# The ninth step of a layer 1 batch: each product of the next k ahead of its mixing

## The chip, the core and the metric

The kernel runs on one core of a Trainium2 chip. The metric is the device time of one execution in microseconds (us). The core has five engines with an instruction queue each: TensorE (PE; its weight loads are listed apart as PEld), VectorE (DVE), ScalarE (ACT), GpSimd (POOL) and SyncE (SP), which here only issues transfers (DMA). An engine works through its queue in the order in which the program gives it, and waits at an instruction until the semaphores that it names have been reached. Work in SBUF is fed to TensorE, whose results stand in PSUM until another engine takes them away.

## The reference, cut to what matters

Eight images of 512 channels and 1024 positions go through two attention layers. The change lies in layer 1, which is computed batch by batch, a batch being one image:

```python
xf = x.reshape(b, c, t)                                  # c = 512, t = 1024, after a group norm
q = jnp.einsum('oc,bct->bot', w_q, xf).reshape(b, heads, hd, t)      # 8 heads of 64
k = jnp.einsum('oc,bct->bot', w_k, xf).reshape(b, heads, hd, t)
v = jnp.einsum('oc,bct->bot', w_v, xf).reshape(b, heads, hd, t)
attn = jnp.einsum('bhdq,bhdT->bhqT', q, k) * scale
attn = jnp.einsum('gh,bhqT->bgqT', w_head, attn)         # the heads are mixed
attn = jax.nn.softmax(attn, axis=-1)
mean, var = moments of attn over both last axes
attn = (attn - mean) / jnp.sqrt(var + EPS) * in_gamma + in_beta
out = jnp.einsum('bhqT,bhdT->bhqd', attn, v).reshape(b, t, c) @ w_proj.T + b_proj
```

(The line of the moments is shortened.) All of it is float32. The kernel doesn't divide by the softmax sums at once: it multiplies the values with plain exponentials and brings in sums and moments later.

## The kernel before, in words

**Steps.** In layer 1 a batch has eight blocks of 128 query positions, p = 0 to 7. A block goes through four stages: its scores; their mixing over heads with the exponentials; a transpose with statistics; and the product with v ("values"). `Attention1.step(p, t, ag)` (L1847) writes out one quarter t = 0 to 3 of step p. In step p the scores of block p, the mixing of block p - 1 and the values of block p - 2 (from the third quarter on those of block p - 1) stand side by side, so that there is a ninth step, p = 8, in which there are no new scores. The order of these calls is the order of each engine's queue: it is written out by hand, and no scheduler changes it.

**One mixing.** The scores are copied from PSUM to `raw`, and `regroup` (L1642) has SyncE move them to other partitions, into `re` (L1646). `mix(p, s)` (L1656) reads `re` with matmuls on 32 x 32 tiles of the array (L1665) into two PSUM tiles of the pool `ps_m`; ScalarE then writes the exponentials `e` (L1678), one instruction for each tile. `flip` (L1693) transposes `e` into `et` on VectorE, `moments` (L1704) takes its statistics there, `values` (L1720) multiplies `et` with v on TensorE, and `leave` (L1736) takes the results away on ScalarE. `sums` (L1746 to L1750, VectorE) and `totals` (L1757, TensorE, tile `z`) make the softmax sums.

**The next k.** While a batch ends, the k of the next one is computed: 512 x 512 weights by 512 x 1024 positions, as seven block products instead of eight (a scheme of Strassen's kind). `Projection.products(m)` (L1367) issues product m as four matmuls of 128 x 128 by 512 (L1379; the profile lists eight, two for each matmul), and `leave(m)` (L1385) takes it out of PSUM: product 1 is copied to a sum `u` on ScalarE (L1388); product 2 is added on top of product 1 in the same PSUM tile, after that copy, and leaves on ScalarE as a quarter of k (L1433); product 6 is added to `u` on VectorE (L1394), product 7 makes a second sum `v` there (L1396), product 5 is added to `u` (L1400) and makes a quarter of k with `v` (L1435), as do 4 and 3. The right factors of products 5 to 7 and 4 are differences of blocks of y that VectorE makes (L1354); 0 and 1 of them are made at the end of the first quarter, 2 and 3 at the end of the second.

**The agenda.** An `Agenda` holds functions under slots, and `ag.run(slot)` calls those of a slot. The batch loop (L1922 to L1998) puts products 1, 2, 6 and 7 under 31.5, 32.5, 33.5 and 34.5, which `step` calls in the ninth step at 4p - 0.5 to 4p + 2.5. `k_go` (L1941) issues a product and notes its leaving in `due`; `k_leave` (L1441) issues what is noted at the end of the same quarter, ahead of that quarter's `flip` and `moments`. After the ninth step come product 5, the rest of the values, products 4 and 3, v, the output projection and the next q. The eighth batch has no next k, and nothing stands under these slots.

**PSUM.** The pool `ps_m` has three buffers of two banks. Scores, mixings (two each), products of projections and pairs of v take them in the order of the program; a matmul into a buffer waits until its last contents have been read. Values and `z` use another pool of two buffers.

Of the kernel before, what the change touches and what calls it, by code (L numbers as in the profile page):

```python
# [467 lines left out]
def tile_two_attention_layers(  # L468
# [228 lines left out]
    with ExitStack() as l0:  # L697
# [505 lines left out]
        for b in range(B):  # L1203
            more = b + 1 < B
            ag = Agenda()
# [61 lines left out]
    with ExitStack() as l1:  # L1267
# [173 lines left out]
        def k_leave():  # L1441
            for fn in due:
                fn()
            due.clear()
# [168 lines left out]
        class Attention1:  # L1613
# [233 lines left out]
            def step(self, p, t, ag):  # L1847

                new, old, older = p < NT, p >= 1, p >= 2
                if t == 0:  # L1850
                    if new:
                        for i in range(3):
                            self.scores(p, i)
                    if older:
                        self.values(p - 2, 0, 2, 3)
                        self.leave(p - 2, 0)
                        self.sums(p - 2)
                        if p % 2 == 0 and p >= 4:
                            self.divide(p // 2 - 2, nc.gpsimd)
                    if old:  # L1860
                        self.mix(p - 1, 0)
                    ag.run(4 * p - 0.5)
                elif t == 1:
                    if older:
                        self.values(p - 2, 1, 0)
                        self.flip(p - 1, 0)
                        self.totals(p - 2)
                        self.moments(p - 1, 0)
                    if new:
                        self.scores(p, 3)  # L1870
                    if old:
                        self.mix(p - 1, 1)
                    ag.run(4 * p + 0.5)
                elif t == 2:
                    if older:
                        self.values(p - 2, 1, 1)
                    if new:
                        self.scores(p, 4)
                        self.scores(p, 5)
                    if old and not new:  # L1880
                        self.mix(p - 1, 2)
                    ag.run(4 * p + 1.5)
                    if older:
                        self.values(p - 2, 1, 2, 3)
                        self.leave(p - 2, 1)
                    if old and new:
                        self.mix(p - 1, 2)
                else:
                    if new:
                        self.scores(p, 6)  # L1890
                        if old:
                            self.values(p - 1, 0, 0)
                        self.scores(p, 7)
                        if old:
                            self.mix(p - 1, 3)
                            self.values(p - 1, 0, 1)
                    else:
                        self.mix(p - 1, 3)
                        self.values(p - 1, 0, 0, 1)
                    ag.run(4 * p + 2.5)  # L1900
                k_leave()
                if p == 1 or old and t:
                    self.flip(p - 1, t)
                    self.moments(p - 1, t)
                if new:
                    for kh, s in (
                        (), ((0, 0), (0, 1), (0, 2)), ((0, 3),), ((1, 0), (1, 1), (1, 2), (1, 3)),
                    )[t]:
                        self.regroup(p, kh, s)
                if old and t == 0:  # L1910
                    self.piece()
                ag.run(4 * p + t)
# [9 lines left out]
        for b in range(B):  # L1922
            more = b + 1 < B
            a = Attention1(b)
            ag = Agenda()
# [143 lines left out]
```

## Time and profile before

| | |
|---|---|
| median of 3 runs | 3999.17 us (3997.65 to 4006.88) |
| the profiled execution | 3999.31 us, span 3997.5 us |
| TensorE busy | 3885.5 us, 97% of the span |
| VectorE busy | 2834.6 us, 71% |
| ScalarE busy | 1971.3 us, 49% |
| mixing, all of it (L1665) | 315.3 us busy, 19.3 us idle ahead of it |
| values, all of it (L1720) | 557.0 us busy, 12.1 us idle ahead of it |
| first matmul of product 1, first and seventh batch | 1982.95 and 3652.95 us |

A row of a timeline gives the start from the beginning of the span, the duration, engine, line, operation, the tiles written and read, the number of instructions merged in it, and in brackets how long the engine was idle ahead of it and what ended that. Matmuls are pipelined, so the end of a group overlaps the start of the next by about a tenth of a microsecond; sums are made from start to start. "PEclk" is the share of TensorE's full clock that was granted.

### The profile page before, as it was taken

The page shows a single profiled execution, that of the slowest core. Times are in us where ns is not written, and L with a number is a line of the kernel's source. Part 1 is how long each engine was busy: PE and PEld are TensorE (multiplying, and loading weights), DVE is VectorE, ACT ScalarE, POOL GpSimd, SP SyncE. Part 2 cuts the span into 40 slices and gives each one's busy share as a digit, 9 for nine tenths or more (in the row PEclk, how much of TensorE's full clock was granted, in tenths as well). Part 3 has the DMA queues.
Part 4 walks back from the last instruction along what each step waited for, and adds up shares of the span by engine and source line. Part 5 has one row for each costly group of instructions (what it writes and reads, how often), then busy time and mean ns, then how long its engine had stood idle before and what let it go on. Part 6 is the DMA issues. An engine that isn't in the chain of part 4 may idle for free.

```text
span 3997.5 us, 95841 instructions
## 1 busy us (share of the span) xinstructions
PE 3885.5 (97%) x41932; PEld 1826.1 (46%) x41932; DVE 2834.6 (71%) x4124; ACT 1971.3 (49%) x2431; POOL 128.5 (3%) x150
## 2 busy tenths in 40 slices
PE   8999999999999999999999999999999999999997
PEld 4353535344343535344544535545545445445354
DVE  4748475766657584857958949859769679588597
ACT  1726363544536271615717528437257166175274
POOL 0000000000000000000100000000001000000010
PEclk9999999999999999999999999999999999999999
DMA  3313131111121111217828749658469288397384
GB/s 121 120 48 117 46 120 48 62 59 66 53 83 54 72 68 61 75 66 184 230 92 226 190 120 237 173 137 227 148 164 228 99 210 207 97 232 198 107 219 127
DMA packets 245883, 519.10 MB, mean 130 GB/s; under 512 B 47312, under 2 KB 54480, under 8 KB 238800
## 3 DMA queue, kind: packets, MB, share of 16 engines
q1 hardware_dynamic: 238912, 497.95, 43.2%
q0 software_dynamic: 6544, 14.94, 1.7%
q8 instruction: 331, 5.42, 0.6%
q14 instruction: 96, 0.79, 0.1%
HBM read 197.16 MB, written 46.92 MB: 61 GB/s over the span
## 4 chain that ended last, share of the span: by engine, by line
PE 81%; DVE 13%; ACT 2%; DMA 2%; issue 2%; SPq 0%; DVEq 0%
PE s L1084 11%; PE a L1110 11%; PE a L1720 7%; PE s L1628 7%; DVE bn L1704 6%; PE pk_p L902 6%; PE pq_p L902 5%; PE pv L1454 5%; PE pv_p L902 5%; DVE et L1693 5%; PE pp_p L902 5%; PE pk L1379 4%; PE pq L1379 4%; PE pp L1379 4%; PE m L1665 4%
## 5 line engine op out<-in xcount | busy, mean ns | idle before, releaser
L1693 DVE STREAM_TRANSPOSE et<-e 128x2048 f32<-128x2048 f32 x256 | 587.3, 2294 | 88.7 <-ACT e L1678 86.8
L1720 PEld LDWEIGHTS a<-et,v 128*64 128x64 f32 x16384 | 509.2, 138 | 296.2 <-issue 247.6
L1704 DVE BATCH_NORM_STATS2 bn<-e 128x6 f32<-128x512 f32 x1024 | 634.3, 675 | 0.0
L1089 ACT ACTIVATE e<-s 128x1024 f32<-128x1024 f32 x512 | 497.2, 1026 | 234.5 <-PE s L1084 232.1
L1640 ACT COPY raw<-s 128x1024 f32<-128x1024 f32 x480 | 470.2, 1018 | 226.1 <-PE s L1628 197.5
L1720 PE MATMUL a<-et,v 128*64 128x64 f32 x16384 | 557.0, 225 | 12.1 <-DVE et L1693 11.4
L1678 ACT ACTIVATE e<-m 128x1024 f32<-128x1024 f32 x512 | 496.2, 1021 | 126.5 <-PE m L1665 54.2
L1097 DVE TENSOR_TENSOR zacc<-zacc,e 128x1024 f32<-128x1024 f32 x384 | 468.7, 1221 | 87.2 <-ACT e L1089 64.9
L1628 PE MATMUL s<-k,q 64*64 64x512 f32 x4096 | 516.0, 608 | 6.2 <-DVE q L1493 3.1
L1084 PE MATMUL s<-q,k 64*64 64x512 f32 x4096 | 490.1, 593 | 2.3 <-ACT e L1089 2.3
L1110 PE MATMUL a<-e,v 64*64 64x512 f32 x4096 | 484.1, 589 | 0.0
L1665 PE MATMUL m<-re,wmix 32*32 32x512 f32 x8192 | 315.3, 604 | 19.3 <-DMA re<-raw 17.8
L1110 PEld LDWEIGHTS a<-e,v 64*64 64x64 f32 x4096 | 156.7, 133 | 282.8 <-issue 282.2
L1084 PEld LDWEIGHTS s<-q,k 64*64 64x64 f32 x4096 | 147.9, 133 | 275.2 <-issue 240.7
L1628 PEld LDWEIGHTS s<-k,q 64*64 64x64 f32 x4096 | 127.7, 132 | 220.8 <-issue 78.2
L1454 PE MATMUL pv<-wv,y 128*128 128x512 f32 x480 | 212.1, 597 | 0.0
L1736 ACT COPY q<-a 64x256 f32<-64x256 f32 x256 | 93.7, 366 | 184.7 <-PE a L1720 182.7
L1772 POOL DMA_DIRECT2D zd<-rz x56 | 34.7, 619 | 3449.0 <-DVE r L1784 3449.0
L1454 PEld LDWEIGHTS pv<-wv,y 128*128 128x128 f32 x480 | 89.3, 190 | 116.9 <-issue 110.3
L1665 PEld LDWEIGHTS m<-re,wmix 32*32 32x32 f32 x8192 | 66.7, 103 | 148.9 <-ACT raw L1640 58.6
L1458 ACT COPY v<-pv 128x512 f32<-128x512 f32 x30 | 17.6, 585 | 218.7 <-PE pv L1454 218.7
L1095 DVE TENSOR_TENSOR zacc<-e,e 128x1024 f32<-128x1024 f32 x64 | 78.3, 1223 | 56.1 <-ACT e L1089 56.1
(315 smaller groups left out, 3942.4 us busy)
## 6 DMA issues: line engine op xcount, KB each, us to landing
re<-raw SPq DMA_DIRECT2D x1024, 256.0 KB
left_q<-left_q SPq DMA_DIRECT2D x17, 1792.0 KB
left_p<-left_p SPq DMA_DIRECT2D x17, 1792.0 KB
left_k<-left_k SPq DMA_DIRECT2D x10, 1792.0 KB
x<-in_x_dram SPq DMA_DIRECT2D x32, 512.0 KB
rzb<-zd SPq DMA_DIRECT2D x128, 128.0 KB
x<-x SPq DMA_DIRECT2D x64, 256.0 KB
y<-x SPq DMA_DIRECT2D x32, 512.0 KB
```

The lines of the kernel that those rows point to most:

```text
L902: nc.tensor.matmul(out, st, mv, start=start, stop=(k == 1), skip_group_check=True)
L1084: nc.tensor.matmul(ps[c * D : c * D + D, m], k[r, hp, k0 : k0 + D], q[r, hp, ts(f, FB)], start=True, stop=True,)
L1089: nc.scalar.activation(e[i], ps, AF.Exp, scale=S0 * S0)
L1110: nc.tensor.matmul(acc[g][a][m * D : m * D + D], v[rows, kc, ts(2 * hp + m, D)], e[i][rows, m], start=(kc == 0), stop=(kc == NG - 1),)
L1379: nc.tensor.matmul(self.ps[m][:, i], w[:, left, k * HC + i * P : k * HC + i * P + P], right[:, k], start=(k == 0 and m != 2), stop=(k == 1 ...
L1454: nc.tensor.matmul(ps[:, m], y_t[b][:, c, ts(2 * i + m, P)], w[:, c], start=(c == 0), stop=(c == NCC - 1),)
L1628: nc.tensor.matmul(ps[c * D : c * D + D, m], qo_t[b][r, p, hp, ts(c, D)], k_t[b][r, hp, ts(kh, FB)], start=True, stop=True,)
L1665: nc.tensor.matmul(ps[a // 2][c * 32 : c * 32 + 32, a % 2].rearrange("p (r h k) -> p h r k", r=2, h=2), wmix[rows].rearrange("p g i -> p ( ...
L1678: nc.scalar.activation(e[:, :, 2 * h : 2 * h + 2].rearrange("p r a k -> p a r k"), ps[h].rearrange("p a (r k) -> p a r k", r=2), AF.Exp,)
L1693: nc.vector.transpose(self.et[p, u].rearrange("p kb (r st a) g q -> p st kb r (a g q)", r=2, st=2)[:, st], self.e[p, s].rearrange("p r a ( ...
L1704: nc.vector.bn_stats(self.bn[p][:, s, a], e[:, :, a].rearrange("p r k -> p k r"))
L1720: nc.tensor.matmul(acc[two * D : two * D + D, s].rearrange("p (x q) -> p x q", q=4), v_t[b][:, kb, ts(g, D)], et[:, kb, :, g], start=(kb = ...
```

## The change

In the four quarters of a step the call of the agenda's slot is put ahead of the mixing. In the fourth quarter it goes ahead of the mixing and of the values behind it, and it is called in the branch without new scores alone. Slots at these places hold work in the ninth step only, so nothing else moves. `k_leave` keeps its place, and so the queues of ScalarE, VectorE, GpSimd and SyncE keep their orders.

```diff
                         if p % 2 == 0 and p >= 4:
                             self.divide(p // 2 - 2, nc.gpsimd)
+                    ag.run(4 * p - 0.5)
                     if old:
                         self.mix(p - 1, 0)
-                    ag.run(4 * p - 0.5)
                 elif t == 1:
...
                     if new:
                         self.scores(p, 3)
+                    ag.run(4 * p + 0.5)
                     if old:
                         self.mix(p - 1, 1)
-                    ag.run(4 * p + 0.5)
                 elif t == 2:
...
                         self.scores(p, 4)
                         self.scores(p, 5)
+                    ag.run(4 * p + 1.5)
                     if old and not new:
                         self.mix(p - 1, 2)
-                    ag.run(4 * p + 1.5)
                     if older:
...
                     else:
+                        ag.run(4 * p + 2.5)
                         self.mix(p - 1, 3)
                         self.values(p - 1, 0, 0, 1)
-                    ag.run(4 * p + 2.5)
                 k_leave()
```

In the ninth step TensorE's queue then reads as follows (v for the values, with the number of records that the profile shows for them):

```
before: mixing 0, product 1, v 32, z, mixing 1, product 2, v 32, mixing 2, product 6, v 64,
        mixing 3, v 64, product 7, product 5, v 192, z
after:  product 1, mixing 0, v 32, z, product 2, mixing 1, v 32, product 6, mixing 2, v 64,
        product 7, mixing 3, v 64, product 5, v 192, z
```

## The prediction

> **What bounds the kernel now.** I read the page's busy shares first, then the waits of TensorE, then the ninth step (p = 8) of the batches as a timeline, engine by engine. The shares say that TensorE is nearly always at work, so time comes only from its few waits:
>
> ```profile
> PE 3885.5 (97%) x41932; PEld 1826.1 (46%) x41932; DVE 2834.6 (71%) x4124; ACT 1971.3 (49%) x2431; POOL 128.5 (3%) x150
> L1665 PE MATMUL m<-re,wmix 32*32 32x512 f32 x8192 | 315.3, 604 | 19.3 <-DMA re<-raw 17.8
> ```
>
> The mixing waits 17.8 us in all for the transfer that regroups the scores. The first batch's ninth step on TensorE (start, duration; the bracket is idle time before it):
>
> ```profile
> 1981.87 1.15 PE L1665 MATMUL m<-re,wmix 32*32 32x512 f32 x32 [1.69 <-DMA re<-raw]
> 1982.95 3.70 PE L1379 MATMUL pk<-y,left_k 128*128 128x512 f32 x8
> 1986.58 1.15 PE L1720 MATMUL a<-et,v 128*64 128x64 f32 x32
> 1987.56 0.37 PE L1757 MATMUL z<-sel,zz 128*64 128x32 f32 x4
> 2003.45 7.13 PE L1379 MATMUL pk<-right,left_k 128*128 128x512 f32 x16
> 2010.51 5.82 PE L1720 MATMUL a<-et,v 128*64 128x64 f32 x192
> 2016.16 0.37 PE L1757 MATMUL z<-sel,zz 128*64 128x32 f32 x4
> ```
>
> Only mixing 0 waits; from there to 2016.16 TensorE has no other gap, and the chain that ended last runs along it. In the seven batches with a following one this wait is 1.69, 2.40, 1.86, 1.41, 3.29, 2.33 and 2.51 us, 15.49 us together: all that the change can take away directly. ScalarE and VectorE in the same step:
>
> ```profile
> 1983.20 1.94 ACT L1678 ACTIVATE e<-m 128x1024 f32<-128x1024 f32 x2 [2.24 <-issue]
> 1986.69 1.01 ACT L1388 COPY re<-pk 128x1024 f32<-128x1024 f32 x1 [1.55 <-PE pk L1379]
> 1993.68 2.28 DVE L1693 STREAM_TRANSPOSE et<-e 128x2048 f32<-128x2048 f32 x1
> 1998.28 1.20 DVE L1354 TENSOR_TENSOR right<-y 128x1024 f32<-128x1024 f32 x1
> 2003.90 2.45 DVE L1704 BATCH_NORM_STATS2 bn<-e 128x6 f32<-128x512 f32 x4
> 2007.19 1.22 DVE L1396 TENSOR_TENSOR re<-re,pk 128x1024 f32<-128x1024 f32 x1 [0.84 <-PE pk L1379]
> ```
>
> To be seen: the copy of product 1 (L1388) stands behind the two exponentials of mixing 0, and product 7's departure (L1396) stands at the end of a VectorE run without gaps from 1993.68 to 2006.35.
>
> **What the Trainium skill says.** "TensorE: Matmul & The Clock Gate", Part 3 (what overlaps and what doesn't): matmuls start and end strictly in program order. So what stands behind a waiting product waits too; the gapless order above agrees. The same page, Part 1 (the HAM clock gate): a free-running window of 3413 ns measures activity, and after an idle window the array runs at half clock. The trace agrees and sharpens it. The clock records hold halvings of 3.41 us or twice that; counted in windows of that length, every window of layer 1 with 1.83 us or more of TensorE idle is followed by half clock, and none with 1.74 or less:
>
> ```profile
> 2810.36:2813.77 3.41, 1.58 (x40) 1.00 1.00 255
> 2813.78:2817.18 3.40, 3.40 (x4) 0.50 1.06 242
> 3373.56:3376.97 3.41, 1.68 (x34) 1.00 0.94 241
> 3376.98:3380.38 3.40, 3.40 (x20) 1.00 1.07 249
> ```
>
> (Columns: window, length, TensorE busy, clock, DMA.) Two of the seven waits cost such a window: in the fourth batch product 1 took 5.40 us for 3.70 (1.70 lost), in the fifth mixing 0 took 1.62 for 1.15 and product 1 4.88 for 3.70 (1.65 lost).
>
> **The change part by part.** No instruction is added or removed, and the orders of ScalarE, VectorE, GpSimd and SyncE stay as they are; only TensorE's order changes, in seven of eight batches. Products 1, 2, 6 and 7 go ahead of mixings 0, 1, 2 and 3; product 7 also passes 64 values (as the trace counts them). PSUM buffers go round differently with it.
>
> I work from T = 1980.13 of the first batch, where TensorE became free, in steps from the rows' starts: product 3.63, mixing 1.07, 32 values 0.98 to 1.05, 64 values 2.02, z 0.30; mixing start to its exponentials 1.34; the pair occupies ScalarE for 1.82; copy 1.01; 0.05 to 0.15 from a releaser's end to TensorE's start, as its other waits show.
>
> *Removed.* Product 1 needs nothing that is late and covers 3.63 us; the longest wait is 3.29, so all seven go: 15.49 plus 0.05 each, 15.8 us. Without this cover they would be back in full.
>
> *Added, before product 2.* It accumulates on product 1's PSUM and so must follow the copy L1388. Until now 32 values, z and mixing 1 stood between them, 2.35 us from product 1's end (1986.58) to 1988.93, while the copy took 1986.69 to 1987.70: no wait. Now: product 1 at 0, mixing 0 at 3.63, exponentials at 4.97, copy at 6.79 to 7.80, product 2 at 7.85. TensorE has only 32 values and z after mixing 0 and is free at 5.98: a wait of 1.87. Behind it stand mixing 1, its exponentials and VectorE's transpose of them.
>
> *Added, before product 6.* Mixing 1 starts at 11.48, exponentials at 12.82; product 6's buffer comes free with the first of them at 13.84, and TensorE is free at 13.58: 0.31.
>
> *Added, before product 7.* The late exponentials end at 14.76, so the transpose at 1993.68 (13.55 from T) starts at 14.80. VectorE then needs 4.60 to its third subtraction (1993.68 to 1998.28) and 1.20 for it: 20.60, against TensorE free at 20.61: about 0.1.
>
> *Added, before product 5.* Until now its buffer came from an exponential. Now it is that of product 7, given back by L1396 on VectorE, behind the statistics of mixing 2. From the third subtraction to the end of those statistics is 8.05 (1998.28 to 2006.35 less the usual overlap): L1396 runs 27.45 to 28.67, product 5 starts at 28.75; TensorE is free at 27.42: 1.33. Behind it stand the remaining 192 values, z and the tail of the batch.
>
> *Moved.* Products 7 and 5 stood together (7.06); apart they are 7.26, 0.2 more. What one change of kind from product to mixing costs, the trace doesn't show; the nearest, product to values, is 0.2 and is in my 3.63. Four such changes a batch at a price of 0 take 0.8 us off it (5.6 in all, 4004), at 0.4, twice the nearest, they add as much (4016); I keep 0.2.
>
> Sum: z at 32.38 + 5.65 = 38.03 from T instead of 34.29 plus the old wait, so 3.75 added per batch: 7 x 3.75 = 26.2. Net 26.2 - 15.8 = +10.4 us. Nothing downstream absorbs it: after z TensorE runs without a gap through products 4 and 3, values of v, output and q.
>
> *Half clock.* The two old windows go: -3.35. The new wait before product 2 shows as 1.80 us idle, right at the threshold; it counts only if it falls whole into one window, with a chance of (3.41 - 1.80)/3.41 = 0.47. Bounds are 0 and 7 windows of 1.7 us; I take two, +3.4. Total +10.5 on the profiled execution: 3999.31 + 10.5 = 4009.8. That execution is 0.14 above the median of 3999.17 (its span 3997.5 lies 1.8 under its own time), so **4010 us**.
>
> **The rivals.**
> *The product-5 wait stays hidden.* If VectorE caught up, 1.33 x 7 = 9.3 would fall away: about 4000.5, no change. For it: VectorE is 71% busy overall. Against it: it is gapless in just this stretch.
> *More half clock.* With four or more windows, or dearer changes of kind: 4014 to 4021. For it: seven idle stretches at the threshold. Against: each needs luck in phase.
> *Faster.* The waits before products 2 and 5 don't reach TensorE, because the copy and the sum come early enough; then 0.4 us of waits and 0.2 of change of kind remain per batch: 3999.2 - 15.8 - 3.35 + 4.2 = 3984. It decides where the new waits stay under 1.0 us per batch ((15.8 + 3.35 - 12)/7). Against it: both releasers stand in in-order queues behind work that itself waits for mixings now later.
> *Nothing happens.* Excluded for seven batches by the program's order, certain for the eighth, which has no next k.
>
> **How the numbers follow.** I call 0.3%, 12 us, what a measurement of this kernel tells from no change; the line is 4011.2. The case as worked, with one to three windows (4006 to 4014): 0.5, of which 0.24 lie above the line. No new window (4004 to 4007): 0.10. More half clock: 0.24. Product-5 wait hidden: 0.10. Faster: 0.06. Slower: 0.24 + 0.24 = 0.48; same 0.26 + 0.10 + 0.10 = 0.46; faster 0.06. The range 4003 to 4018 leaves out the hidden and the faster case and the tail of the heavy one; the likeliest case has 4006 to 4014.
>
> **What would show it.** In the changed profile: no wait of the mixing for the regrouping in the ninth step of seven batches; before product 2 an idle of about 1.8 us ended by L1388; before product 6 about 0.3 by an exponential; before product 5 about 1.3 by L1396; from product 1 to z 38.0 us in each batch, whatever the transfer did. The forecast is wrong if the wait before product 2 is under 1 us, or if half clock follows most of the seven.

## The result, and the profile after

The changed kernel takes 4010.6 us (median of 19 runs, 4005.05 to 4016.79), against 4000.74 us for the kernel before in runs beside it (19 runs, 3994.13 to 4010.3). The ratio is 1.002, with a 95% interval of 1.0013 to 1.0026: slower, by 5 to 10 us. The profiled execution has a span of 4009.7 us, against 3997.5 before.

The page of the changed kernel, its busy shares and the group of the mixing (busy, mean ns of one | idle ahead of it):

```profile
PE 3889.8 (97%) x41932; PEld 1824.7 (46%) x41932; DVE 2836.8 (71%) x4124; ACT 1969.2 (49%) x2431; POOL 128.5 (3%) x150
L1665 PE MATMUL m<-re,wmix 32*32 32x512 f32 x8192 | 316.6, 608 | 6.3 <-DMA re<-raw 4.0
```

The mixing's wait for the regrouping has shrunk from 17.8 us to 4.0, and none of the rest lies in the ninth step of the seven batches with a following one. Three waits of the products are listed in its place among TensorE's waits in the changed kernel (us in total, times, longest):

```profile
PE pk L1379 <- ACT re L1388: 12.5, 7, 1.8
...
PE pk L1379 <- DVE re L1396: 8.2, 7, 1.2
...
PE pk L1379 <- ACT e L1678: 1.4, 7, 0.2
```

Each of them stands once in each of the seven batches. Here is the first batch's ninth step on TensorE, in the changed kernel (start, duration, and in brackets the idle time ahead and what ended it):

```profile
1979.41 3.70 PE L1379 MATMUL pk<-y,left_k 128*128 128x512 f32 x8
1983.05 1.14 PE L1665 MATMUL m<-re,wmix 32*32 32x512 f32 x32
1984.12 1.15 PE L1720 MATMUL a<-et,v 128*64 128x64 f32 x32
1985.10 0.37 PE L1757 MATMUL z<-sel,zz 128*64 128x32 f32 x4
1987.28 3.70 PE L1379 MATMUL pk<-y,left_k 128*128 128x512 f32 x8 [1.82 <-ACT re L1388]
1990.91 1.14 PE L1665 MATMUL m<-re,wmix 32*32 32x512 f32 x32
1991.99 1.15 PE L1720 MATMUL a<-et,v 128*64 128x64 f32 x32
1993.34 3.70 PE L1379 MATMUL pk<-right,left_k 128*128 128x512 f32 x8 [0.20 <-ACT e L1678]
...
2008.14 3.70 PE L1379 MATMUL pk<-right,left_k 128*128 128x512 f32 x8 [1.17 <-DVE re L1396]
...
2017.42 0.37 PE L1757 MATMUL z<-sel,zz 128*64 128x32 f32 x4
```

Product 1 starts as soon as TensorE is free, and mixing 0 follows without a gap. Then product 2 stands still for 1.82 us. From product 1 to z it is 2017.42 - 1979.41 = 38.01 us. The copy that product 2 waits for, on ScalarE of the changed kernel:

```profile
1984.39 1.94 ACT L1678 ACTIVATE e<-m 128x1024 f32<-128x1024 f32 x2 [4.11 <-issue]
1986.21 1.02 ACT L1388 COPY re<-pk 128x1024 f32<-128x1024 f32 x1
```

Product 1 is finished at 1983.1, but its copy starts only at 1986.21, behind the exponentials of the mixing that now follows product 1. And the sum that product 5 waits for, on VectorE:

```profile
2002.26 2.30 DVE L1693 STREAM_TRANSPOSE et<-e 128x2048 f32<-128x2048 f32 x1
2004.48 2.48 DVE L1704 BATCH_NORM_STATS2 bn<-e 128x6 f32<-128x512 f32 x4
2006.88 1.20 DVE L1396 TENSOR_TENSOR re<-re,pk 128x1024 f32<-128x1024 f32 x1
```

Product 7's result lay ready from about 2003.9 (product 7 started at 2000.22 and took 3.67); its departure L1396 took its place in the queue, behind a transpose and the statistics, and ended at 2008.08, 0.06 before product 5's start.

I call the time from the end of the last values ahead of the ninth step to the start of its last z the *step length*. In the profile before, without half clock, it is 36.54 us on average; in the changed kernel 37.94 to 37.96 in each of the six batches without half clock in this step. Seven times the difference is 9.8 us.

### The profile page after: what moved, and what is told of

Its sections match the earlier page's. It is cut to its first block, busy times and chain, and to the rows that moved or that the text cites. A ratio compares the mean times of both kernels' runs of the same rounds, so it can differ in the third digit from the quotient of the medians.

```text
span 4009.7 us, 95848 instructions
## 1 busy us (share of the span) xinstructions
PE 3889.8 (97%) x41932; PEld 1824.7 (46%) x41932; DVE 2836.8 (71%) x4124; ACT 1969.2 (49%) x2431; POOL 128.5 (3%) x150
## 5 line engine op out<-in xcount | busy, mean ns | idle before, releaser
L1458 ACT COPY v<-pv 128x512 f32<-128x512 f32 x30 | 17.6, 585 | 218.7 <-PE pv L1454 218.7
```

## The experiments

All of them were timed beside the kernel before on the same chip, in two sets. The first has "product 1 alone", "products 1, 2 and 6", "the copies ahead of the exponentials" ("copies early" in what follows) and "the gap of mixing 1 filled" ("gap filled") (before: 4003.36 us, 28 runs); the second has "product 7 alone", "the sum ahead of the statistics" ("sum early") and the two repeated profiles (before: 4003.71 us, 25 runs). The diffs are against the kernel before unless it is said otherwise.

### Product 1 alone

```diff
+                    ag.run(4 * p - 0.5)
                     if old:
                         self.mix(p - 1, 0)
-                    ag.run(4 * p - 0.5)
```

> Product 1 alone stands ahead of its mixing; products 2, 6 and 7 follow theirs as before. From the start of product 1 to the last z of the step the kernel before took 34.29 us plus the transfer's wait (2.26 on average), the changed one 38.0. Theory A (what the change costs are the new waits for queued copies and buffers before products 2, 6, 7 and 5): the transfer's wait is covered here too, and only about 1.0 us comes back, because mixing 1 now waits for the second exponential of mixing 0 (its buffer) and product 2 for its copy; no wait before products 6, 7 and 5. 35.3 us per batch, 9 to 12 us faster than before, about 3990. Rival B (the loss is TensorE's half clock, set off by new idle stretches): the copy's wait is nearly the same as in the changed kernel, so the time stays within 5 us of it, 4005 to 4015. Rival C (putting products next to mixings is itself dear): no gain over before.

Measured: 3980.82 us (3980.25 to 3985.41), ratio 0.9952 (0.9939 to 0.9964), so 19 us faster (14 to 24). TensorE in its first ninth step:

```profile
1979.50 3.70 PE L1379 MATMUL pk<-y,left_k 128*128 128x512 f32 x8
1983.13 1.14 PE L1665 MATMUL m<-re,wmix 32*32 32x512 f32 x32
...
1985.55 2.05 PE L1665 MATMUL m<-re,wmix 32*32 32x512 f32 x32
1986.47 0.23 PEld L1665 LDWEIGHTS m<-re,wmix 32*32 32x32 f32 x28 [0.78 <-ACT e L1678]
1987.54 3.70 PE L1379 MATMUL pk<-y,left_k 128*128 128x512 f32 x8
```

The transfer's wait is gone, and no TensorE matmul row has a bracket in its place. (The row of the weight loads, PEld, is from the timeline of all engines.) Mixing 1 takes 1.99 us from start to start (1985.55 to 1987.54) for the usual 1.07: its second PSUM tile waits for the second exponential. In the matmuls this shows as a longer row and not as a gap; in the weight loads the last 28 of 32 come behind a gap of 0.78 us, which the exponential ended. The step length is 35.19 in all seven batches, 1.35 less than before. So in step length the first of the four moves holds all of the gain, and the other three cost more than it brings (37.94 - 35.19 = 2.75). The step came out as expected; the time gained is larger than the 9 to 12 us expected, which "Waits and clock together" takes up. The two rivals, no gain and a time near the changed kernel's, fell.

### Products 1, 2 and 6

As the changed kernel, with product 7 left where it was (the first three hunks of the diff).

> Products 1, 2 and 6 ahead of their mixings, product 7 behind mixing 3 and its values as before. Theory A: the wait before product 2 (1.8 us shown) and before product 6 (0.2) stay. The wait before product 5 goes, but mixing 3 now takes the buffer of product 6, which VectorE gives back only behind its transpose, statistics and two subtractions: mixing 3 can start 22.95 us from product 1's start instead of 20.6, a wait of 2.3 us ended by L1394. 38.7 us from product 1 to z, 5 us slower than the changed kernel, about 4015. Rival D (moving product 7 is what costs, through product 5's buffer alone): the 1.2 us before product 5 go, 8 us faster than the changed kernel, about 4002.

Measured: 4015.13 us (4010.55 to 4019.64), ratio 1.0029 (1.0017 to 1.0040), step length 38.71. TensorE, first batch:

```profile
1990.06 3.70 PE L1379 MATMUL pk<-y,left_k 128*128 128x512 f32 x8 [1.82 <-ACT re L1388]
...
1996.11 3.70 PE L1379 MATMUL pk<-right,left_k 128*128 128x512 f32 x8 [0.20 <-ACT e L1678]
...
2002.83 1.05 PE L1665 MATMUL m<-re,wmix 32*32 32x512 f32 x4
2005.17 1.14 PE L1665 MATMUL m<-re,wmix 32*32 32x512 f32 x28 [1.29 <-DVE re L1394]
2006.24 2.09 PE L1720 MATMUL a<-et,v 128*64 128x64 f32 x64
```

Mixing 3 now needs the buffer of product 6, which L1394 gives back late on VectorE. From its start to the values behind it are 3.41 us (2002.83 to 2006.24), 2.34 more than 1.07; the bracket shows 1.29 of this. With product 7 in between, as in the changed kernel, mixing 3 has no such wait; so the fourth move, for all that it creates the wait of product 5, is worth 0.77 us per batch once the second and third are made (38.71 - 37.94).

### Product 7 alone

The last hunk of the diff alone.

> Product 7 alone stands ahead of mixing 3 and its values; products 1, 2 and 6 as before. Theory A (the wait before product 5 comes of the late exponentials of mixing 1, which only the earlier products bring, together with product 7's buffer): L1396 ends 27.4 us from the point at which TensorE became free, and TensorE reaches product 5 at 25.2 plus the transfer's wait, so product 5 waits 0.4 to 0.8 us in the batches with a transfer's wait under 2 us and not in the others: about 0.2 us on average and 0.2 for products 7 and 5 apart, 37.0 us against 36.5; 3 us slower than before. Rival D (product 7's move alone brings the wait): 1.2 us before product 5 in all seven, 9 to 10 us slower than before.

Measured: 4003.8 us (12 runs, 3997.26 to 4011.91; the profiled one is the slowest), ratio 1.000 (0.9992 to 1.0009). TensorE's second batch, from product 7 to product 5:

```profile
2283.20 3.70 PE L1379 MATMUL pk<-right,left_k 128*128 128x512 f32 x8
2286.83 1.14 PE L1665 MATMUL m<-re,wmix 32*32 32x512 f32 x32
2287.90 2.08 PE L1720 MATMUL a<-et,v 128*64 128x64 f32 x64
2289.91 3.70 PE L1379 MATMUL pk<-right,left_k 128*128 128x512 f32 x8
```

Product 5 doesn't wait in any batch of this trace. In this batch, where mixing 0 waited 2.31 us for the transfer, the buffer comes back 0.25 us before product 5's start:

```profile
2288.47 1.19 DVE L1396 TENSOR_TENSOR re<-re,pk 128x1024 f32<-128x1024 f32 x1
2290.14 2.31 DVE L1693 STREAM_TRANSPOSE et<-e 128x2048 f32<-128x2048 f32 x1 [0.48 <-ACT e L1678]
```

So the wait before product 5 isn't made by product 7's place alone, and the rival, 1.2 us in all seven batches, fell. L1396 ends 8.01 us after the sum L1354 that product 7 needs, here (2281.65 to 2289.66) as in the changed kernel (2000.07 to 2008.08), while TensorE needs 6.7 us from product 7 to product 5. With products 2 and 6 ahead as well, product 7 starts 0.15 us after that sum, and 1.2 us are missing; here it starts 1.55 us after it.

The expectation of a wait in the batches with a transfer's wait under 2 us remains untested. There are three (1.77, 1.98 and 1.99 us), and in each TensorE fell to half clock in the ninth step, so that it came to product 5 later still, 0.7 us after the buffer. The only two batches without half clock waited 2.31 and 2.39 us for the transfer, and had 0.25 and 0.34 us to spare.

### The copies ahead of the exponentials

The changed kernel, with the departures of products 1 and 2 issued at once, and so ahead of the exponentials of mixings 0 and 1 on ScalarE (diff against the changed kernel):

```diff
                     ag.run(4 * p - 0.5)
+                    k_leave()
                     if old:
                         self.mix(p - 1, 0)
...
                     ag.run(4 * p + 0.5)
+                    k_leave()
                     if old:
                         self.mix(p - 1, 1)
```

> The changed kernel with the copies of products 1 and 2 issued ahead of the exponentials of mixings 0 and 1 on ScalarE (k_leave directly behind the product in the first two quarters). Theory A: product 2 no longer waits for the copy, which ends 4.7 us from product 1's start; the transpose of mixing 1 is back at 13.55. VectorE then sets the pace: product 7 waits about 0.6 for its factor, product 5 about 1.3 for L1396. 36.75 us from product 1 to z, 8 to 9 us faster than the changed kernel, about 4001, the same as before. Rival B: without the idle stretch of 1.8 us the half clock behind it goes, and only that, 2 to 4 us faster than the changed kernel. Rival E (PE's order itself, not ScalarE's queue): no change, 4010.

Measured: 3995.01 us (21 runs), ratio 0.998 (0.9974 to 0.9987), step length 36.61. TensorE, first batch:

```profile
1986.27 3.70 PE L1379 MATMUL pk<-y,left_k 128*128 128x512 f32 x8
...
1999.78 3.67 PE L1379 MATMUL pk<-right,left_k 128*128 128x512 f32 x8 [0.94 <-DVE right L1354]
...
2007.70 3.70 PE L1379 MATMUL pk<-right,left_k 128*128 128x512 f32 x8 [1.17 <-DVE re L1396]
```

The wait before product 2 is gone in all seven batches, which shows its cause: the place of the copy behind the exponentials, and nothing about product 2 itself. About half of it comes back (0.94 to 1.00 us in six batches, 0.36 in one) before product 7, for a VectorE sum (L1354) that was 0.1 late in the changed kernel and that TensorE now reaches sooner. The wait before product 5 stays as it was, since product 7 still starts right behind that sum.

### The sum ahead of the statistics

The changed kernel, with the statistics of mixing 2 in the ninth step moved behind L1396 on VectorE (diff against the changed kernel):

```diff
                 k_leave()
+                if not new and t == 3:
+                    self.moments(p - 1, 2)
...
-                    self.moments(p - 1, t)
+                    if new or t != 2:
+                        self.moments(p - 1, t)
```

> The changed kernel with one move on VectorE: in the ninth step the statistics of mixing 2 stand behind the sum of product 7 (L1396) instead of ahead of it. Theory A: L1396 then ends about 26.4 us from product 1's start, before TensorE is free at 27.4, so the wait before product 5 (1.17 us shown) goes and nothing takes its place: 36.75 us from product 1 to z, 8 to 9 us faster than the changed kernel, about 4002. Rival F (product 5 is held by its transferred factor or by the pool's order, not by L1396): the wait stays and the time with it, 4010.

Measured: 3997.69 us (13 runs), ratio 0.999 (0.9982 to 0.9999), step length 36.70. The row of product 5 in the first batch has no bracket any more, while that of product 2 keeps its own:

```profile
1989.40 3.70 PE L1379 MATMUL pk<-y,left_k 128*128 128x512 f32 x8 [1.82 <-ACT re L1388]
...
2009.03 3.70 PE L1379 MATMUL pk<-right,left_k 128*128 128x512 f32 x8
```

The wait before product 5 is the queue ahead of L1396, and it costs the 1.24 us of step length that go with it (37.94 - 36.70).

### The gap of mixing 1 filled

Product 1 ahead of mixing 0, and 32 values that stood behind product 2 moved ahead of mixing 1 (diff against "product 1 alone"):

```diff
                 elif t == 1:
...
+                    if older and not new:
+                        self.values(p - 2, 1, 1)
                     if old:
                         self.mix(p - 1, 1)
...
                 elif t == 2:
-                    if older:
+                    if older and new:
                         self.values(p - 2, 1, 1)
```

> Product 1 ahead of mixing 0; between z and mixing 1 stand the 32 values that followed product 2 before, so that mixing 1 and product 2 find their buffer and copy ready; products 6 and 7 as before. Theory A: no wait longer than 0.2 us from product 1 to z, 34.4 to 34.6 us, so nearly the whole of the transfer's wait is gained: 15 to 18 us faster than before, about 3984. Rival C or E: no gain over before, or less than the first run of this study.

Measured: 3974.87 us (3974.69 to 3980.79), ratio 0.9937 (0.9925 to 0.9950): 25 us faster than the kernel before, and the best kernel of this study. The step length is 34.28, and TensorE waits for nothing in the ninth step:

```profile
1985.04 1.13 PE L1720 MATMUL a<-et,v 128*64 128x64 f32 x31
1986.10 1.16 PE L1665 MATMUL m<-re,wmix 32*32 32x512 f32 x32
1987.19 3.70 PE L1379 MATMUL pk<-y,left_k 128*128 128x512 f32 x8
```

Mixing 1 takes 1.09 from start to start again. 34.28 is thus TensorE's work in this step, in this order, without waits: 7 x (36.54 - 34.28) = 15.8 us below the kernel before. That equals the 15.8 us that the prediction put on the transfer's waits.

### Both kernels profiled once more

> The kernel before once more, for a second trace. Theory A: the same waits for the transfer of 1.4 to 3.3 us, give or take one, since they come of the order of the queues; the rest of layer 1 is 234.5 us of work and 5 to 7 us of waits from one ninth step to the next in every kernel; what differs is the number of half-clock windows, 2 to 8 in layer 1 up to its last batch, as their free-running phase falls. Rival G (the run order, not chance, sets the half clock): the windows are at the same places as in the first trace.

> The changed kernel once more, for a second trace. Theory A: 37.94 us in every ninth step without half clock, as in the first trace, with the same four waits to 0.1 us; the half-clock windows are elsewhere and of another number. Rival G: the windows are at the same places.

Measured: 3999.38 and 4008.18 us. The kernel before waits for the transfer for other times than in its first profile (2.05, 2.25, 2.09, 1.38, 3.53, 2.16 and 2.45 us, 15.91 together). The changed kernel again has 37.93 or 37.94 in six batches, and 39.63 in one, the third this time. The rival, half clock at the same places in both traces, holds in part: some places come again (near 2812, 3092 and 3331 us in the kernel before, 2221 in the changed kernel), others don't. The changed kernel's new waits come from its own program order, and repeat; the old one came from a transfer, and varies.

### Waits and clock together

Four of the kernels came out faster than their step lengths give, and than was expected of them: product 1 alone (3981 us, expected 3990), copies early (3995, expected 4001), gap filled (3975, expected 3984) and sum early (3998, expected 4002). For product 1 alone, 7 x 1.35 makes 9.5 us, and measured are 19.

Each run has a recorded mean clock. A window of 3.41 us at half clock cost a product 1.70 us (5.40 for 3.70), so I take half clock to lose (1 - clock) x span. The 53 runs of the kernel before bear this out among themselves: a straight line through their spans against this loss has a slope of 1.01 (correlation 0.88). With the means over all runs of each kernel (before: 0.9946 in 53 runs):

| kernel | step length, us | seven steps against before, us | mean clock | half clock against before, us | sum, us | measured, us (95%) |
|---|---|---|---|---|---|---|
| changed kernel | 37.94 | +9.8 | 0.9949 | -1.5 | +8.3 | +8.0 (5 to 10) |
| product 1 alone | 35.19 | -9.5 | 0.9966 | -8.2 | -17.6 | -19.2 (-24 to -14) |
| products 1, 2, 6 | 38.71 | +15.2 | 0.9956 | -3.9 | +11.2 | +11.6 (7 to 16) |
| product 7 alone | 36.87 | +2.3 | 0.9952 | -2.1 | +0.2 | 0.0 (-3 to +4) |
| copies early | 36.61 | +0.5 | 0.9966 | -8.2 | -7.7 | -8.0 (-10 to -5) |
| gap filled | 34.28 | -15.8 | 0.9968 | -9.0 | -24.8 | -25.2 (-30 to -20) |
| sum early | 36.70 | +1.1 | 0.9962 | -6.1 | -4.9 | -4.0 (-7 to 0) |

Step lengths are of one profile, without half clock; "measured" is the ratio less one, times 4003 us. The clocks are recorded to a thousandth, which is 4 us, and each mean is over 5 to 28 runs. The loss of before is that of its runs in the same set, 21.7 us in the first and 21.4 in the second. For the runs beside the changed kernel no clock of the kernel before is on record, so it stands against the first set. Of the +2.3 of product 7 alone, 1.4 come from longer waits for the transfer in its one trace, 16.87 us against 15.49.

The sums fall within 1.6 us of what the ratios give. Differences of the medians are further off for the two kernels with five runs each, -22.5 us for product 1 alone and -28.5 for gap filled, and +9.9 for the changed kernel; from these the sums are up to 5 us away.

So two things move these kernels: the waits in the ninth step, and how often TensorE falls to half clock. Where a long idle time in the ninth step goes altogether (product 1 alone, gap filled) or is at most 1.2 us (copies early), the loss to half clock is 8 to 9 us smaller. Only a part of this lies in the ninth step itself, as the counts in the last section show. The longest idle time alone doesn't decide: "sum early" keeps its 1.82 us, and yet loses 6 us less to half clock than the kernel before.

## Why the prediction was right

It said 4010 us and came out at 4010.6. That the two are so close is in part luck: the prediction stood on a median of 3999.17 us from three runs and added 10.8, while beside the changed kernel the kernel before took 4000.74 us, 9.9 less. Its working can be held against the trace step by step.

*Removed, 15.8 us: right.* No mixing of these ninth steps waits for the transfer in the changed kernel, and "product 1 alone" shows the removal by itself.

*Wait before product 2, 1.87 worked, 1.80 as shown: right, with its cause.* It shows as 1.82, and is gone when the copy goes ahead of the exponentials.

*Wait before product 6, 0.31: 0.20 shown. Before product 7, about 0.1: 0.09 to 0.11.* The first is ended by the exponential, as named; the second isn't in the list of waits, but product 7 starts 0.14 to 0.15 us after the end of its sum L1354 in all seven batches.

*Wait before product 5, 1.33: 1.17 shown,* behind the statistics as worked, and gone when these go behind L1396. It is 1.24 of step length. I had worked 8.07 us from the sum that product 7 needs to the end of L1396 (20.60 to 28.67), and measured are 8.01; that the wait hangs on product 7 starting right behind that sum is what "product 7 alone" adds.

*Change of kind at 0.2: right.* Product to mixing is 3.64 from start to start (1979.41 to 1983.05), the 3.63 that I had carried over from product to values. Product 1 to z: 38.03 worked, 38.01 measured.

*Half clock: the balance right, the parts not.* I let two windows go and two come, +0.05 in all. The clocks of all runs say -1.5 us. The chance of 0.47 for each wait before product 2 did not come out: the four traces with this wait (the changed kernel twice, products 1, 2, 6 and sum early) have half clock behind 4 of the 28. That I took two windows, and not the three that 0.47 gives, was judgement. Each of the two traces of the changed kernel has one window in these steps, and in both the rest lies outside: in the profiled pair the six stretches between the steps grew from 1446.86 to 1452.81 us, of which 5.1 is half clock (10.25 lost against 5.12). This made that pair 12.2 apart in span: +8.2 in the steps, +5.9 in the stretches between, and -1.9 in what lies ahead of the first and behind the last. It is one execution against one, and the medians do not carry it.

The sentence on the threshold was too sharp. Even in the trace that it was read from, a window at half clock itself, from 3332.59 us on, was followed by another after 1.13 us idle. In the changed kernel's trace (window, length, TensorE busy, PEld, DVE, ACT, POOL, clock, DMA share, GB/s):

```profile
1985.72:1989.13 3.41, 1.85 (x5) 0.89 (x6) 3.38 (x3) 1.51 (x2) 0.00 (x0) 1.00 0.97 273
1989.14:1992.54 3.40, 3.40 (x55) 1.32 (x55) 3.33 (x10) 0.28 (x1) 0.64 (x1) 1.00 0.84 247
2265.61:2269.02 3.41, 1.59 (x53) 1.35 (x38) 3.12 (x6) 2.84 (x3) 0.00 (x0) 1.00 1.07 255
2269.03:2272.43 3.40, 3.40 (x5) 1.32 (x6) 3.33 (x8) 0.00 (x0) 0.58 (x1) 0.50 0.99 311
2781.03:2784.44 3.41, 1.70 (x52) 1.29 (x36) 3.31 (x8) 2.60 (x5) 0.00 (x0) 1.00 1.06 263
2784.45:2787.85 3.40, 3.40 (x43) 0.62 (x41) 3.33 (x8) 1.01 (x1) 0.64 (x1) 0.50 0.47 123
```

The first and second pair are the same wait of 1.82 us in two batches. In the first it is cut by the window's edge (1.56 idle in the window), and the clock stays; in the second it falls whole into one window, and product 2 runs at half clock:

```profile
2268.91 5.40 PE L1379 MATMUL pk<-y,left_k 128*128 128x512 f32 x8 [1.82 <-ACT re L1388]
```

That is the phase argument of the prediction at work. The third pair is another wait, 38 us ahead of the ninth step, in a place that the change doesn't touch:

```profile
2784.19 0.40 PE L1757 MATMUL z<-sel,zz 128*64 128x32 f32 x4 [1.71 <-DVE zz L1750]
```

It has half clock behind 1.71 us, under the 1.74 that I had put on the safe side, and the second profile of the kernel before has a window of 1.98 us idle with none after it:

```profile
2532.26:2535.67 3.41, 1.44 (x50) 1.29 (x46) 3.41 (x4) 1.33 (x3) 2.35 (x1) 1.00 0.94 222
2535.68:2539.08 3.40, 3.30 (x37) 1.43 (x38) 3.33 (x7) 1.94 (x2) 0.00 (x0) 1.00 1.04 275
```

*The rivals.* "The product-5 wait stays hidden" fell: it stands in all seven batches. "More half clock" fell: one window for seven waits in each trace, and a clock no lower than before. "Faster" fell because both releasers kept their places behind late work; what the change gives with both waits removed was not run: "copies early" and "sum early" take away one each, and "product 1 alone", which has neither (3981 us), makes only one of the four moves.

## What to carry to other kernels

In this kernel, moving a product ahead of the work that waits for a transfer paid once, for the one that covers the wait; each further product that was moved ahead needed its PSUM buffer, or the copy that it builds on, earlier than the engine that gives it back got to it. So follow each moved matmul to what gives its buffer back, and ask what stands ahead of that in its engine's queue: waits of 1.87 and 1.33 us per batch were worked from the trace of the kernel before, and 1.82 and 1.17 came. And look at the granted clock beside the waits: every window of 3.41 us with 2.0 us or more of TensorE idle was followed by half clock in these traces, which costs 1.7 us more.

## What the runs showed of the hardware that was not expected

Of the half clock, "TensorE: Matmul & The Clock Gate" in the Trainium skill, Part 1 (the HAM clock gate), says that the slow state comes after one idle window or more. In these traces a window need not be idle: 1.71 us of 3.41 was enough in the changed kernel, 1.72 and 1.77 in two others. In the stretch of layer 1, from 1850 to 3900 us, every window of the ten traces with 2.0 us or more was followed by half clock, those between 1.6 and 1.99 in part, and none below 1.6 unless it was at half clock itself. What decides in between, these runs don't show.

Here is where the windows at half clock lie in that stretch (a record of twice the length counts as two):

| trace | longest waits in the ninth step, us | windows in the ninth step | windows ahead of it |
|---|---|---|---|
| kernel before, two traces | transfer, 1.4 to 3.5 | 2 and 4 | 3 and 3 |
| product 7 alone | transfer, 1.8 to 3.2 | 5 | 4 |
| changed kernel, two traces | copy, 1.8 | 1 and 1 | 6 and 4 |
| products 1, 2, 6 | copy, 1.8 | 1 | 4 |
| sum early | copy, 1.8 | 1 | 2 |
| copies early | sum, 1.2 | 0 | 1 |
| product 1 alone | no gap | 0 | 1 |
| gap filled | no gap | 0 | 2 |

The windows in the ninth step follow its waits, and are gone where no wait is over 1.2 us: at 1.7 us each, 3.4 to 6.8 us of the kernel before. Those ahead of it all come 36 to 41 us before the ninth step, behind one wait that every kernel has: in the seventh step z waits for a sum on VectorE (L1750) or an exponential, 0.8 to 2.1 us in each batch. They are most of the windows of the changed kernel. Why there are only one or two of these in the last four kernels of the table, one trace of each doesn't show; with it the rest of the 8 to 9 us in the clock column remains open.

A stall can hide in a row. Mixing 1 of "product 1 alone" lost 0.92 us without a bracket on the matmuls, because only its second tile waited: the row's time from start to start and the row of the weight loads showed it, and filling it was worth 0.91 us a batch (35.19 - 34.28).
